# A convolution and attention block on one core: another opening order, half of a norm on ScalarE, position terms by accumulating transfer, and a Strassen product with one addition fewer

## The chip, the core and the metric

The kernel runs on one core of a Trainium2 chip. The metric is the device time in microseconds of a whole execution. Every ratio below was timed on one chip in one job, the kernels alternating. The runs belong to four such jobs, in which the kernel before took 2318.69, 2319.20, 2318.54 and 2318.88 us (medians), so times of different jobs are comparable to about 0.7 us. All runs named here count as fast: none was more than 1.5% above the fastest of its kernel. Ratios are the mean time of one kernel's fast runs over that of the other's of the same rounds, so they are not quite the ratio of the medians that are quoted.

## The reference, cut to what matters

```python
def cbs(x, w, p, pad):                       # convolution, batch norm, silu
    return jax.nn.silu(bn_eval(conv2d(x, w, pad), p))

def bot_attention(x, qkv_w, rw, rh):         # 4 heads of 64, 1024 positions
    ...
    r = (rw + rh).reshape(1, HEADS, HD, hw)  # position terms
    logits = einsum('bhdi,bhdj->bhij', q, k + r) * HD ** -0.5
    ...
t = cbs(x, cv1_w, cv1_bn, 0)                 # 1x1, 512 -> 512 channels
ys = [t[:, :C], t[:, C:]]                    # C = 256
for i in range(2):
    z = cbs(ys[-1], m_cv1_w[i], m_cv1_bn[i], 1)          # 3x3
    z = bot_attention(z, m_qkv_w[i], m_rw[i], m_rh[i])
    z = silu(bn_eval(conv2d(z, m_cv2_w[i], 0), m_cv2_bn[i]))
    ys.append(ys[-1] + z)
return cbs(concatenate(ys, axis=1), cv2_w, cv2_bn, 0)
# the result of the kernel: x + block(group_norm(x)), x of 8 images of 512 x 32 x 32
```

## The kernel before

The eight images follow each other. While one is in its first attention, the next one is loaded and normalised, and its first 1x1 convolution (cv1) begins behind that attention. The group norm is a generator, advanced one step at a time from places inside the attention. Its last step is on VectorE:

```python
def apply(cs, gm, gr):
    for c in cs:
        last = nc.vector.tensor_scalar(xts[c], xts[c], gm[:, c : c + 1], gr[:, c : c + 1],
                                       ALU.subtract, ALU.mult)
    return last
...                                       # two yields with statistics, one with the mean
yield apply(range(NX), gm, gn_rstd(dev)[0])   # the power in gn_rstd runs on GpSimd
```

An attention has four groups of four pairs. Each pair makes two logits tiles in PSUM, where the matmuls write (three buffers, shared with most other products), takes their exponential on ScalarE, sums it on VectorE, and multiplies by the values on TensorE one pair later:

```python
for i, (_, j) in enumerate(pair):
    ps = ps_big.tile([P, 2, HALF], F32, tag="big", name="l_ps")   # 3 buffers
    ...                                                           # 4 matmuls
    exp = nc.scalar.activation(pt[:, i], ps, AF.Exp, scale=SCALE)
```

From the second image on, cv1 is a Strassen product of seven products:

```python
def begin():
    ...                                        # t1, t2, t3, t4 on VectorE, two halves each
        tt(t4[:, c], t2[:, c], b21[c], ALU.subtract)
    kept["ps"] = product(a11, b11)
    kept["m1"] = to(spare("xr", 2), kept["ps"])   # to(): a copy on ScalarE
    to(y0_2, product(s4, b22))
...
def rest():
    kept["m5"] = to(spare("xr", 2), product(s1, t1))
    kept["m6"] = to(spare("x", NX), product(s2, t2))
    to(y1_2, product(s3, t3))
    to(y1_1, product(a22, t4))
```

The opening loads the first x tile, then a raw block of 3x3 weights, then the second x tile, and puts one weight transform ahead of the norm's mean on VectorE:

```python
xs = [load_x(act, 0, 0, NX)]
...
raws = {(0, 0, 0): load_raw(0, 0, 0, "k")}
xs.append(load_x(act, 0, 1, NX))
...
with tc.issue_after(shifted.ins):              # batch-norm constants
    nc.gpsimd.tensor_scalar(rstd, bnp[:, :, 3], BN_EPS, None, ALU.add)
    nc.gpsimd.tensor_tensor(rstd, rstd, mhalf[:, :NBN], ALU.pow)
    nc.gpsimd.tensor_tensor(sh, bnp[:, :, 0], rstd, ALU.mult)
    ...
```

## Time and profile before

| | before |
|---|---|
| time, median of the first three runs | 2318.8 us |
| profiled span | 2317.9 us |
| TensorE busy | 2288.9 us (99%) |
| VectorE, ScalarE, GpSimd busy | 1838.3, 987.4, 94.8 us |
| TensorE's listed waits in the first 81 us | 19.4 us in seven |
| after that | one of 0.5 us |
| after the last matmul of the last convolution started | 9.7 us |

Read it from TensorE down: an engine that is busy for 99% of the span sets the time, and the others count only where TensorE waits for them. The lines themselves are in the prediction below.

### The profile page before, as it was taken

To read this page: it belongs to the slowest core of one execution; us is meant where nothing else is said; L and a number is where in the kernel's file an instruction comes from. 1 tells how busy PE (TensorE), PEld (TensorE's weight loads), DVE (VectorE), ACT (ScalarE), POOL (GpSimd) and SP (SyncE) were. 2 spreads that over 40 slices of the span, in tenths; PEclk is the share of its full clock that TensorE was granted. 3 is DMA by queue.
4 is the path that set the end of the run, shared out by engine and by line. 5 is a ranking of instruction groups with operands and counts; after the bars stand their busy time and mean duration, and the time that the engine had idled before them with its cause. 6 is when DMAs were issued, how large, how long until landed. Compare 5 with 4: busy or idle time off the path is not lost.

```text
span 2317.9 us, 36534 instructions
## 1 busy us (share of the span) xinstructions
PE 2288.9 (99%) x14806; PEld 1174.6 (51%) x14806; DVE 1838.3 (79%) x2914; ACT 987.4 (43%) x1292; POOL 94.8 (4%) x314
## 2 busy tenths in 40 slices
PE   7999999999999999999999999999999999999998
PEld 4547346463554636446364553645436364473643
DVE  7887977888788887888788887888877988777774
ACT  2443624536244352544525345253542535335352
POOL 2000000000000000000000000000000000000000
PEclk9999999999999999999999999999999999999999
DMA  7422234041430415213161221602216031260201
GB/s 240 172 86 87 107 111 189 16 150 33 143 145 15 150 34 187 105 36 125 51 221 53 69 94 50 250 29 94 67 47 250 29 128 33 70 226 15 87 11 62
DMA packets 95521, 235.60 MB, mean 102 GB/s; under 512 B 28016, under 2 KB 50736, under 8 KB 81904
## 3 DMA queue, kind: packets, MB, share of 16 engines
q1 hardware_dynamic: 83600, 182.84, 23.1%
q0 software_dynamic: 11744, 50.34, 5.7%
q8 instruction: 119, 1.95, 0.3%
q14 instruction: 58, 0.48, 0.1%
HBM read 198.54 MB, written 34.60 MB: 101 GB/s over the span
## 4 chain that ended last, share of the span: by engine, by line
PE 96%; DVE 3%; POOL 0%; ACT 0%; DMA 0%; issue 0%; SPq 0%; DVEq 0%; POOLq 0%; ACTq 0%
PE av_ps L769 19%; PE l_ps L735 19%; PE c_ps L971 14%; PE c L1029 8%; PE p_ps L631 8%; PE x_ps L1141 6%; PE c_new L1029 6%; PE m_ps L995 5%; PE ps L387 4%; PE pv_ps L635 3%; PE s_ps L787 1%; PE p_ps L635 1%; PE s_ps L805 1%; DVE acc L755 0%; DMA raw<-in_m_cv_w_dram 0%; PE v_ps L596 0%
## 5 line engine op out<-in xcount | busy, mean ns | idle before, releaser
L739 ACT ACTIVATE pt<-l_ps 128x1024 f32<-128x1024 f32 x512 | 494.9, 1023 | 410.1 <-PE l_ps L735 385.5
L755 DVE TENSOR_TENSOR acc<-acc,pt 128x1024 f32<-128x1024 f32 x384 | 469.3, 1222 | 65.7 <-ACT pt L739 39.9
L769 PE MATMUL av_ps<-pt,vT 64*64 64x512 f32 x4096 | 486.5, 592 | 0.5 <-DVE ao L777 0.5
L735 PE MATMUL l_ps<-q,kr 64*64 64x512 f32 x4096 | 486.0, 591 | 0.0
L971 PEld LDWEIGHTS c_ps<-v_in,u 128*128 128x128 f32 x2720 | 306.0, 192 | 6.7 <-issue 6.7
L971 PE MATMUL c_ps<-v_in,u 128*128 128x128 f32 x2720 | 306.2, 275 | 0.0
L769 PEld LDWEIGHTS av_ps<-pt,vT 64*64 64x64 f32 x4096 | 159.3, 133 | 269.3 <-issue 223.1
L735 PEld LDWEIGHTS l_ps<-q,kr 64*64 64x64 f32 x4096 | 160.2, 133 | 263.2 <-issue 252.0
L453 ACT COPY m<-c_ps 128x256 f32<-128x256 f32 x96 | 35.4, 368 | 220.6 <-PE c_ps L971 218.3
L1029 PE MATMUL c_new<-t_in,ws 128*128 128x512 f32 x288 | 124.6, 592 | 0.0
L995 PE MATMUL m_ps<-ao,m_sb 128*128 128x512 f32 x256 | 112.5, 592 | 0.0
L370 ACT ACTIVATE m_kept<-m_kept,bh,sh 128x512 f32<-128x512 f32 x42 | 31.9, 806 | 146.0 <-DVE m_kept L1113 86.3
L753 DVE TENSOR_TENSOR acc<-pt 128x1024 f32<-128x1024 f32 x64 | 78.0, 1219 | 18.2 <-ACT pt L739 18.0
L1029 PEld LDWEIGHTS c_new<-t_in,ws 128*128 128x128 f32 x288 | 54.8, 190 | 68.8 <-issue 66.0
L631 PE MATMUL p_ps<-t_z,sq 128*128 128x512 f32 x180 | 87.2, 593 | 0.0
L370 ACT ACTIVATE t<-m_ps,bh,sh 128x512 f32<-128x512 f32 x64 | 48.0, 775 | 83.9 <-PE m_ps L995 82.5
L995 PEld LDWEIGHTS m_ps<-ao,m_sb 128*128 128x128 f32 x256 | 48.7, 190 | 61.2 <-issue 61.2
L1003 DVE TENSOR_TENSOR ylast<-t,ypad 128x512 f32<-128x512 f32 x32 | 22.0, 692 | 63.2 <-ACT t L370 63.2
L370 ACT ACTIVATE z<-z,bh,sh 128x512 f32<-128x512 f32 x64 | 48.6, 806 | 54.4 <-DVE z L482 54.4
L446 DVE TENSOR_TENSOR v_in<-w_rows 128x512 f32<-128x512 f32 x96 | 65.5, 683 | 0.0
L454 DVE TENSOR_TENSOR r_mid<-c_ps,m 128x256 f32<-128x256 f32 x64 | 27.0, 422 | 48.4 <-ACT m L453 48.3
L1029 PE MATMUL c<-ypad,ws 128*128 128x512 f32 x144 | 63.8, 592 | 0.0
(255 smaller groups left out, 3004.7 us busy)
## 6 DMA issues: line engine op xcount, KB each, us to landing
u<-u SPq DMA_DIRECT2D x85, 1024.0 KB
x<-in_x_dram SPq DMA_DIRECT2D x32, 512.0 KB
x_res<-in_x_dram POOLq DMA_DIRECT2D x32, 512.0 KB, 6.9
out_dram<-m_kept POOLq DMA_DIRECT2D x28, 512.0 KB, 7.4
u<-u_new POOLq DMA_DIRECT2D x12, 1024.0 KB, 4.9
w<-in_cv_w_dram SPq DMA_DIRECT2D x12, 1024.0 KB
rs<-r_dram SPq DMA_DIRECT2D x96, 128.0 KB
ws<-s SPq DMA_DIRECT2D x24, 512.0 KB
```

What stands on the lines that cost most here:

```text
L370: return nc.scalar.activation(dst, src, AF.Silu, scale=sh[:, k : k + 1], bias=bh[:, k : k + 1])
L387: last_product[0] = nc.tensor.matmul(ps[:, half, :], w_of(k), rhs_of(k, half), start=(k == begin), stop=(k == end))
L631: nc.tensor.matmul(ps[:, o, :], w[:, o, :], rhs, start=not onto, stop=True, skip_group_check=onto)
L635: nc.tensor.matmul(v[:, ts(j, P)], rhs[:, ts(j, P)], w[:, 2, :], start=j == 0 and not onto, stop=True, skip_group_check=True,)
L735: nc.tensor.matmul(ps[kh * HD : (kh + 1) * HD, hd, :], kr[r, c, o : o + HD], q[r, c, ts(half, HALF)], start=True, stop=True,)
L739: exp = nc.scalar.activation(pt[:, i], ps, AF.Exp, scale=SCALE)
L755: ins = nc.vector.tensor_tensor(accs[g], accs[g], pt[:, i], ALU.add)
L769: nc.tensor.matmul(avs[g][hd * HD : (hd + 1) * HD, kh, :], vT[r, j, o : o + HD], pt[r, i, hd, :], start=(j == 0), stop=(j == NJ - 1),)
L971: nc.tensor.matmul(ps[:, row, col, :], us[i][:, k, row, SLOT[col], :], vs[i][:, k, row, col, :], start=(k == 0), stop=(k == NM - 1),)
L995: nc.tensor.matmul(pss[oc][:, half, :], m2_sb[:, n, k, ts(oc, P)], ao[:, k, ts(half, HALF)], start=(k == 0), stop=(k == NM - 1),)
L1029: nc.tensor.matmul(ps[:, o, :], w[:, k, ts(o, P)], rhs[part][:, c, :], start=(k == 0 and not onto), stop=(k == KB - 1), skip_group_check=onto,
L1141: nc.tensor.matmul(ps[:, o, :], w[:, c, ts(o, P)], rhs[c], start=(c == 0 and not onto), stop=(c == 1), skip_group_check=onto,)
```

## The change

The intent was to start the first matmul sooner, to take work off VectorE (half of the norm's last step, additions of position terms, one addition of the Strassen sums), and to free the last output from a buffer. Cut to its core:

```diff
-    xs = [load_x(act, 0, 0, NX)]
+    xs = [load_x(act, 0, c, NX) for c in range(NX // 2)]
...
-    xs.append(load_x(act, 0, 1, NX))           # it stood behind the raw weights
...
-    with tc.issue_after(loaded.ins):
-        made = make_u(2, u_first[2][:, 0], raws[0, 0, 0])
     with tc.issue_after(read.ins):
+        with tc.issue_after(loaded.ins):
+            made = make_u(2, u_first[2][:, 0], raws[0, 0, 0])
         next(norm)
...                                        # constants: all but the power to VectorE, and behind
...                                        # the power a weight transform that stood further back
-        nc.gpsimd.tensor_tensor(sh, bnp[:, :, 0], rstd, ALU.mult)
+        nc.vector.tensor_tensor(sh, bnp[:, :, 0], rstd, ALU.mult)
...                                        # the norm's last step
-            yield apply(range(NX), gm, gn_rstd(dev)[0])
+            gr = gn_rstd(dev)[0]
+            shift = small.tile([P, 2], F32, tag="dev", name="shift")
+            nc.vector.scalar_tensor_tensor(shift, gm[:, :2], -1.0, gr[:, :2], ALU.mult, ALU.mult)
+            apply(range(2, NX), gm, gr)
+            for c in range(2):
+                nc.scalar.activation(
+                    xts[c], xts[c], AF.Identity, scale=gr[:, c : c + 1], bias=shift[:, c : c + 1]
+                )
+                yield
...                                        # position terms, built once in image 2 (make_r)
+                nc.gpsimd.dma_start(kr[:, 1, :], r_dram, accum_op=ALU.add)
...                                        # Strassen
-                to(y0_2, product(s4, b22))
+                kept["ps5"] = product(s1, [t1[:, c] for c in range(2)])
+                kept["m5"] = to(spare("xr", 2), kept["ps5"])
...
-                to(y1_2, product(s3, t3))
-                to(y1_1, product(a22, t4))
+                ps = product(s3, t3)
+                to(y1_2, ps)
+                to(y1_1, product(a22, t4, ps))      # adds onto ps
...                                        # last output
-                    t = act.tile([P, size], F32, tag="h" if n and final else "t", name="t", bufs=2)
+                    t = act.tile([P, size], F32, tag=("h", "h", "wt")[n] if final else "t", name="t", bufs=2)
```

More of the change, by code (lines that the diff above doesn't have):

```diff
@@ L243, in make_sq, with make_r @@
             nc.gpsimd.dma_start(sq_dram[n][:, 2 * h : 2 * h + 2], t)
+    r_dram = [tc.dram_tile([P, HW], F32, name=f"r{n}") for n in range(N)]
+    def make_r(n):
+        r = act.tile([P, F, F], F32, tag="xr", name="r_new", bufs=2)
+        nc.vector.tensor_tensor(
+            r, rw_sb[:, n, 1, :].unsqueeze(1).to_broadcast([P, F, F]),
+            rh_sb[:, n, 1, :].unsqueeze(2).to_broadcast([P, F, F]), ALU.add,
+        )
+        nc.gpsimd.dma_start(r_dram[n], r.rearrange("p a b -> p (a b)"))
     def load_sq(n):
@@ L551, in apply @@
                 for c in cs:
-                    last = nc.vector.tensor_scalar(
+                    nc.vector.tensor_scalar(
                         xts[c], xts[c], gm[:, c : c + 1], gr[:, c : c + 1], ALU.subtract, ALU.mult
                     )
-                return last
             stats(range(NX // 2))
@@ L562, in group_norm @@
             yield
-            yield apply(range(NX), gm, gn_rstd(dev)[0])
+            gr = gn_rstd(dev)[0]
[5 more added lines that the diff above has]
+                    xts[c], xts[c], AF.Identity, scale=gr[:, c : c + 1], bias=shift[:, c : c + 1]
+                )
+                yield
         def project(n, z):
@@ L610, in first_sum, with project_strassen @@
             return t
-        def project_strassen(n, z, sq, t):
+        def project_strassen(n, z, sq, t, r_dram=None):
             q = act.tile([P, NM, HW], F32, tag="q", name="q")
@@ L704, in later, with attention_fast @@
             def later():
-                for half in range(NH):
-                    add_r(1, half)
+                if r_dram is None:
+                    for half in range(NH):
+                        add_r(1, half)
+            if r_dram is not None:
+                nc.gpsimd.dma_start(kr[:, 1, :], r_dram, accum_op=ALU.add)
             return q, kr, vT, later
-        def attention_fast(n, z, at, behind, sq=None, t=None):
-            q, kr, vT, later = (*project(n, z), None) if sq is None else project_strassen(n, z, sq, t)
+        def attention_fast(n, z, at, behind, sq=None, t=None, r_dram=None):
+            q, kr, vT, later = (*project(n, z), None) if sq is None else project_strassen(n, z, sq, t, r_dram)
             behind.get(-1, lambda: None)()
@@ L1162, in begin @@
                     tt(t3[:, c], b22[c], b12[c], ALU.subtract)
-                    tt(t4[:, c], t2[:, c], b21[c], ALU.subtract)
+                    tt(t4[:, c], b21[c], t2[:, c], ALU.subtract)
                 kept["ps"] = product(a11, b11)
                 kept["m1"] = to(spare("xr", 2), kept["ps"])
-                to(y0_2, product(s4, b22))
+                kept["ps5"] = product(s1, [t1[:, c] for c in range(2)])
+                kept["m5"] = to(spare("xr", 2), kept["ps5"])
             def go_on():
@@ L1173, in rest @@
             def rest():
-                t1, t2, t3, t4 = ([t[:, c] for c in range(2)] for t in kept["t"])
-                kept["m5"] = to(spare("xr", 2), product(s1, t1))
+                _, t2, t3, t4 = ([t[:, c] for c in range(2)] for t in kept["t"])
+                to(y0_2, product(s4, b22, kept["ps5"]))
                 kept["m6"] = to(spare("x", NX), product(s2, t2))
-                to(y1_2, product(s3, t3))
-                to(y1_1, product(a22, t4))
+                ps = product(s3, t3)
+                to(y1_2, ps)
+                to(y1_1, product(a22, t4, ps))
             def add_y0():
@@ L1182, in add_y0 @@
                 tt(y0_2, y0_2, kept["m1"], ALU.add)
-                tt(y0_2, y0_2, kept["m5"], ALU.add)
             def add_y1():
                 tt(y1_2, y1_2, kept["m1"], ALU.add)
-                tt(y1_1, y1_2, y1_1, ALU.subtract)
+                tt(y1_1, y1_1, kept["m1"], ALU.add)
                 tt(y1_2, y1_2, kept["m5"], ALU.add)
@@ L1302 @@
         begin(Y_ORDER[2], range(NX // 2))
-    with tc.issue_after(shifted.ins):
-        nc.gpsimd.tensor_scalar(rstd, bnp[:, :, 3], BN_EPS, None, ALU.add)
+    with tc.issue_after(made.ins), tc.issue_after(shifted.ins):
+        nc.vector.tensor_scalar(rstd, bnp[:, :, 3], BN_EPS, None, ALU.add)
         nc.gpsimd.tensor_tensor(rstd, rstd, mhalf[:, :NBN], ALU.pow)
-        nc.gpsimd.tensor_tensor(sh, bnp[:, :, 0], rstd, ALU.mult)
-        nc.gpsimd.tensor_tensor(bh, bnp[:, :, 2], sh, ALU.mult)
-        nc.gpsimd.tensor_tensor(bh, bnp[:, :, 1], bh, ALU.subtract)
+        made = make_u(0, u_first[0][:, 1], raws[0, 0, 1])
+    with tc.issue_after(made.ins):
+        nc.vector.tensor_tensor(sh, bnp[:, :, 0], rstd, ALU.mult)
+        nc.vector.tensor_tensor(bh, bnp[:, :, 2], sh, ALU.mult)
+        nc.vector.tensor_tensor(bh, bnp[:, :, 1], bh, ALU.subtract)
         for at in bn_m1:
-            nc.gpsimd.tensor_scalar(sh[:, at : at + NM], sh[:, at : at + NM], -1 / 12, None, ALU.mult)
-    with tc.issue_after(made.ins):
-        made = make_u(0, u_first[0][:, 1], raws[0, 0, 1])
-    with tc.issue_after(made.ins), tc.issue_after(applied.ins):
+            last = nc.vector.tensor_scalar(sh[:, at : at + NM], sh[:, at : at + NM], -1 / 12, None, ALU.mult)
+    with tc.issue_after(last.ins), tc.issue_after(applied.ins):
         for i in (1, 2):
@@ L1411 @@
         behind = {g: ahead for g in range(NG)} | {NG: first, NG + 1: second}
+        behind[NG - 1, 1] = lambda: next(norm, None)
         if b > 0:
@@ L1415 @@
             behind[-1] = lambda: make(1, 0, range(PAIRS))
-        ao, check = s.attention_fast(0, z, b * N * NM * NH, behind, sq.get(0), t)
+        if b == 1:
+            behind |= {(NG - 1, n + 1): lambda n=n: (next(norm, None), make_r(n)) for n in range(N)}
+        ao, check = s.attention_fast(0, z, b * N * NM * NH, behind, sq.get(0), t, r_dram[0] if b > 1 else None)
         made = None
@@ L1482 @@
             behind |= {(1, 1): six[3], (2, 1): six[4]}
-        ao, check = s.attention_fast(1, z, (b * N + 1) * NM * NH, behind, sq.get(1), t)
+        ao, check = s.attention_fast(1, z, (b * N + 1) * NM * NH, behind, sq.get(1), t, r_dram[1] if b > 1 else None)
         ylast = act.tile([P, NM, HW], F32, tag="v", name="ylast")
```

## The prediction

> **What bounds the kernel now.** I began with the page: TensorE is busy 2288.9 of 2317.9 us, so at most 29 us of the span is not matmul, whatever the other engines do. Next the view of waits for TensorE, which says where those 29 us are.
>
> ```profile
> span 2317.9 us, 36534 instructions
> PE 2288.9 (99%) x14806; PEld 1174.6 (51%) x14806; DVE 1838.3 (79%) x2914; ACT 987.4 (43%) x1292; POOL 94.8 (4%) x314
> ```
>
> ```profile
> PE gm_ps L497 <- DVE mv L490: 11.0, 1, 11.0
> PE ps L387 <- ACT x L537: 2.7, 1, 2.7
> PE c_ps L971 <- DVE u_new L341: 2.4, 1, 2.4
> PE gv_ps L497 <- DVE dev L509: 0.9, 1, 0.9
> PE ps L387 <- ACT z L370: 0.9, 1, 0.9
> ```
>
> Columns: total wait, number of waits, longest. Every one happens once, in the first 81 us; in the seven images after that TensorE never waits 0.5 us. The remaining 9 us follow the last matmul. So VectorE's 79% and ScalarE's 43% cost nothing in the middle: work taken off VectorE there gains nothing, and work put on another engine can only lose.
>
> The chain that ended last gives the opening, piece by piece (start, length):
>
> ```profile
> 1.49 6.55 DMA raw<-in_m_cv_w_dram
> 9.41 1.26 DVE st L489 x2
> 15.47 5.49 PE ps L387 x6
> 27.04 3.04 POOL rstd L1305
> 30.16 4.58 POOL sh L1306
> 35.35 1.45 ACT ypad L370 x2
> 36.83 0.69 DVE w_tmp L423
> 67.16 5.78 PE c_ps L971 x28
> ```
>
> A raw weight block, loaded ahead of the second x tile, holds that tile's statistics to 9.4. The batch-norm constants take GpSimd from 26.3 to 35.3. Then VectorE runs without a gap from 36.83 to 67.16 (row transforms, weight transforms of the second output half), and TensorE waits on it. Last, the table by stretches; the columns that count are TensorE's and the granted clock before the DMA share:
>
> ```profile
> 0.00:11.00 11.00, 0.00 (x0) 0.00 (x0) 4.23 (x9) 2.10 (x3) 1.93 (x20) 1.00 0.78 257
> 61.90:67.10 5.20, 2.05 (x10) 1.56 (x10) 5.20 (x15) 1.52 (x2) 0.00 (x0) 0.83 0.40 117
> 67.10:73.00 5.90, 5.84 (x31) 5.84 (x32) 3.94 (x12) 0.00 (x0) 1.06 (x2) 0.57 0.65 267
> ```
>
> After the waits of 61.9 to 67.1 the clock falls: 28 matmul passes take 5.78 us there against 0.112 us a pass elsewhere, a further 2.6 us.
>
> **What the Trainium skill says.** "TensorE: Matmul & The Clock Gate", Part 1, says TensorE drops to half clock after an idle window of about 3.4 us and returns after a busy one; the trace agrees (0.57 above). The same page, under "Architectural detail", calls ScalarE's and VectorE's queues strict FIFO; the order of the trace agrees, though in the kernel before no ScalarE instruction stands in the wrong place. "ScalarE: Activation LUTs", "What ACT_TABLE_LOAD costs", gives 186 ns + 0.833 ns per element, 93 ns for each per-partition operand, and says back-to-back ones overlap by 93 ns; for 512 elements with scale and bias that is 0.80 us, and the trace has 0.806 for that silu. For 1024 it gives an estimate of 1.22 us, two in 2.35. "GPSIMD Engine Reference", "Key points", says GpSimd shares SBUF interfaces with VectorE; that fits 4.58 us for a 128x16 multiply beside a busy VectorE, 0.22 us when VectorE was idle.
>
> **The change, part by part.** The instruction order of the changed program (no times in it) decides much here.
>
> *Front.* x tile 2 is now loaded directly behind tile 1. 0.52 MB at the 257 GB/s above is 2.0 us, so it can be used at 4.38 + 2.0 = 6.4; statistics 1.5, then as before to the first big matmul (10.90 to 15.47 = 4.57): 12.4, 3.0 earlier. The constants go to VectorE except the power: VectorE reaches them after the second mean. In the new order the read of the second variance stands before most of a weight transform, so VectorE idles some 1.7 us there; I get row transforms starting at about 32.9 against 36.83 (VectorE, not silu, ends last). From there to the last weight transform TensorE needs for the second output half it has to do the 30.3 us it did before (36.83 to 67.16) plus 0.7 us, two more 384-element transforms less one small one being pulled in front: 64.0, 3.2 earlier. But the new order also puts the first transform of that half late: TensorE reaches it at about 55.0 and gets it at 58.9. One wait of 3.9 us replaces three smaller ones, so the clock should fall once more, for about as long. Gain of the front at the first attention: **3.3 us**.
>
> *Half of the norm's last step on ScalarE.* VectorE saves two of four 1024-element steps (2.98 us for four) in seven images: no gain, it was not waited for. ScalarE gets two activations, and the order places both directly behind the row-sum copy and ahead of the last four exponentials of the attention. They wait for the mean's shift, which needs GpSimd's power. In the second block of image 2:
>
> ```profile
> 431.86 0.38 ACT L793 COPY s_row<-s_ps 128x256 f32<-128x256 f32 x1
> 434.32 1.94 ACT L739 ACTIVATE pt<-l_ps 128x1024 f32<-128x1024 f32 x2 [2.08 <-PE l_ps L735]
> 434.41 1.04 POOL L517 TENSOR_TENSOR gr<-gr,mhalf 128x4 f32<-128x4 f32 x1 [2.69 <-DVE gr L516]
> 435.48 2.98 DVE L552 TENSOR_SCALAR x<-x,gm,gr 128x1024 f32<-128x1024 f32 x4 [1.16 <-POOL gr L517]
> 436.59 1.96 PE L735 MATMUL l_ps<-q,kr 64*64 64x512 f32 x16
> ```
>
> The power ends at 435.45, the shift at 435.65; ScalarE can start at 435.7, two activations take to 438.0, and only then comes the exponential that before began at 434.32; it ends at 439.0. Logits have three PSUM buffers: the second half of the last logits, at 436.59 + 0.86 = 437.45 before, needs the one that this exponential reads. TensorE waits 437.45 to 439.0, 1.55 us, and later steps do not win it back. Seven images (all but the last have a norm behind the attention): **10.9 us lost**.
>
> *Position terms by transfer.* Twelve attentions lose four additions on VectorE: no gain. The accumulating transfer starts when the last of the projections is done, and the second pair's logits come two groups, some 29 us, later; a 512 KB load took 6.9 us. Hidden. Building the terms costs VectorE two 1024-element additions once, in the second image, before the sums for the first product: about **1.1 us lost**, once.
>
> *Strassen.* Still seven products and six copies. One VectorE addition (1.22 us) less in six images: no gain. But the last product now accumulates onto a buffer that is being copied out (1.01 us); five matmuls of the next stage (ten passes of 0.112) are put between. Wait left: 0.04 + 1.01 + 0.03 + latency against 1.12, about 0.13 us; six times, **0.8 us lost**.
>
> *End.* The last block's first half gets another buffer and does not wait for an output transfer (before: 2308.80, 2.44 us after the issue of that transfer). The remaining additions and the three issues move by about **0.8 us** earlier.
>
> Sum: 2318.8 - 3.3 - 0.8 + 10.9 + 1.1 + 0.8 = **2327.5 us**.
>
> **The rivals.** (a) The ScalarE work fits into its idle time (it is busy 57% per pair of exponentials): then only front and end count and the time is about 2316. For it: 1.49 us idle before most exponentials. Against: the two stand back to back and behind a value that is not there until 435.6. (b) TensorE's wait of 1.55 us, if it falls within one clock window, drops the clock each time; up to 1.7 to 3.4 us more in each image, 2340 to 2350. Against: 0.91 us idle at 80 dropped nothing, and the fall at 65 followed 3.9 us of waits. (c) The front's 3 us are lost to the late weight transform and the clock: 2330 to 2331. (d) An accumulating transfer that is several times slower than a plain one would delay the third group of logits in twelve places; it would need over 25 us to show.
>
> **Range and chances.** The activation's length (1.0 to 1.3 us) moves the loss by about 4 us, the front is good for 1 to 5.5 us. I give (a) one chance in ten and (b) one in ten. That makes 2317 to 2334 for 8 in 10. A difference of 2% is 46 us, and no case reaches it: 0.01 faster, 0.97 within 2%, 0.02 slower.
>
> **What would show it.** In the view of waits: a new line of logits waiting for an exponential, some 7 times 1.5 us; ScalarE's norm step waiting for the shift, seven times about 3.5 us. In the opening: first big matmul at 12.4, batch-norm constants ready by 28 and no 4.58 us multiply on GpSimd, row transforms at 33, a wait of some 4 us at 55 to 59 and again a clock of one half. Half the VectorE norm instructions; the second image's product waiting about a microsecond. I am wrong if the logits do not wait, if the front gives more than 6 us, or if attention's third group waits for a transfer.

## The result, and the profile after

The changed kernel took 2328.93 us (median of 6 runs, 2327.23 to 2329.41) against 2318.69 us (6 runs, 2317.74 to 2320.06) for the kernel before: a ratio of 1.0043, with a 95% interval of 1.0030 to 1.0056. It is within 2%, and slower by some 10 us. The profiled spans differ by 10.0 us.

The head of the page of the changed kernel:

```profile
span 2327.9 us, 36547 instructions
PE 2291.4 (98%) x14806; PEld 1167.4 (50%) x14806; DVE 1800.5 (77%) x2861; ACT 1002.7 (43%) x1306; POOL 100.9 (4%) x322
```

VectorE lost 37.8 us of work, as intended, and the program became longer. So look at what TensorE waits for (total us, number, longest):

```profile
PE l_ps L755 <- ACT pt L759: 9.3, 7, 1.3
...
PE c_ps L991 <- DVE u_new L355: 3.2, 1, 3.2
...
PE x_ps L1162 <- DVE t_x L1181: 0.7, 1, 0.7
...
PE c L1049 <- DVE ao L797: 0.3, 1, 0.3
```

The first line is new and happens seven times, once for each image that has a norm behind its first attention. ScalarE's own waits name the cause, seven times too:

```profile
ACT x L577 <- DVE shift L574: 24.1, 7, 3.4
```

The second block of image 2 in order of time (start, length), the same place that the prediction shows of the kernel before:

```profile
431.11 1.04 POOL L527 TENSOR_TENSOR gr<-gr,mhalf 128x4 f32<-128x4 f32 x1 [2.69 <-DVE gr L526]
432.18 0.16 DVE L574 SCALAR_TENSOR_TENSOR shift<-gm,gr 128x2 f32<-128x2 f32 x1 [1.16 <-POOL gr L527]
432.26 1.53 DVE L562 TENSOR_SCALAR x<-x,gm,gr 128x1024 f32<-128x1024 f32 x2
432.38 2.37 ACT L577 ACTIVATE x<-x,shift,gr 128x1024 f32<-128x1024 f32 x2 [3.43 <-DVE shift L574]
434.66 3.74 ACT L759 ACTIVATE pt<-l_ps 128x1024 f32<-128x1024 f32 x4
435.71 1.09 PE L755 MATMUL l_ps<-q,kr 64*64 64x512 f32 x8 [1.32 <-ACT pt L759]
```

ScalarE stands idle for 3.43 us. The first 2.08 us it would have waited for logits anyway, as in the kernel before; for the other 1.35 us logits are ready to be taken, but the two activations are at the head of its queue and their shift is not there. They then take 2.37 us, and only at 434.66 does the first of four exponentials start; TensorE resumes when that one has freed its buffer.

The opening in three views: a line of the chain that ended last, TensorE's row in order of time, and the table by stretches for two clock windows (length; busy time and number of instructions of TensorE, weight loads, VectorE, ScalarE, GpSimd; granted clock; transfer share; GB/s):

```profile
23.73 3.17 POOL rstd L1327
```

```profile
43.26 11.55 PE L991 MATMUL c_ps<-v_in,u_new 128*128 128x128 f32 x102
57.98 0.71 PE L991 MATMUL c_ps<-v_in,u_new 128*128 128x128 f32 x4 [3.17 <-DVE u_new L355]
```

```profile
55.24:58.65 3.41, 0.67 (x4) 0.52 (x4) 3.41 (x11) 0.02 (x1) 0.00 (x0) 1.00 0.00 0
58.65:62.06 3.41, 3.12 (x15) 3.08 (x15) 3.41 (x9) 1.50 (x2) 0.53 (x1) 0.50 0.56 231
```

The first big matmul starts at 12.22 us (before: 15.47), the power ends at 26.9, the row transforms start at 32.0 (before: 36.83), the long wait is there from 54.8 to 58.0, and the clock halves for one window of 3.41 us (before: 6.83 us, from 65.34 to 72.17). The first attention starts at 92.08 instead of 97.35.

**Where the 10 us went.** TensorE runs almost the same matmuls in both kernels, so each one's start can be compared with its twin's. This drift (after minus before) is a staircase that can be read directly:

| piece | drift in us |
|---|---|
| at the first logits of image 1 | -5.27 |
| last logits of the first attention, images 1 to 7 | +1.56 each, 10.9 in all |
| from there to the second attention, images 2 to 7 (Strassen) | +0.35 each, 2.1 in all |
| at the same place in image 2, once more | +1.05 |
| end of image 1 | +0.4 |
| at the last logits of image 8 | 9.11 |
| from the last convolution's last matmul to the end | +0.96 |

After the opening the drift falls by no more than 0.05 us from one logits matmul to the next: what TensorE loses in an image it keeps. In the experiments I use the *body*, the drift between the first logits of image 1 and the last of image 8, because it leaves out the opening. That one scattered by 2 us from run to run under the same code: in the nine runs that have it whole its drift was -4.6 to -6.6 us, with a median of -5.7. The body of the changed kernel is 9.11 + 5.27 = 14.38 us.

### The profile page after: what moved, and what is told of

The parts are those of the page before. It is cut to its first block, busy times and chain, and to the rows that moved or that the text cites. A ratio compares the mean times of both kernels' runs of the same rounds, so it can differ in the third digit from the quotient of the medians.

```text
span 2327.9 us, 36547 instructions
## 1 busy us (share of the span) xinstructions
PE 2291.4 (98%) x14806; PEld 1167.4 (50%) x14806; DVE 1800.5 (77%) x2861; ACT 1002.7 (43%) x1306; POOL 100.9 (4%) x322
## 4 chain that ended last, share of the span: by engine, by line
PE 92%; DVE 4%; issue 1%; ACT 1%; DMA 1%; POOL 1%; SPq 0%; DVEq 0%; POOLq 0%; ACTq 0%
PE l_ps L755 17%; PE av_ps L789 17%; PE c_ps L991 14%; PE c L1049 8%; PE p_ps L648 8%; PE c_new L1049 6%; PE x_ps L1162 6%; PE m_ps L1015 5%; PE ps L397 4%; PE pv_ps L652 3%; PE p_ps L652 1%; PE s_ps L807 1%; DVE acc L775 1%; ACT pt L759 1%; PE s_ps L825 1%
## 5 line engine op out<-in xcount | busy, mean ns | idle before, releaser
L1162 PE MATMUL x_ps<-t_x,sw 128*128 128x512 f32 x144 | 64.1, 594 | 0.7 <-DVE t_x L1181 0.7
```

Source lines behind the costliest of these rows:

```text
L1162: nc.tensor.matmul(ps[:, o, :], w[:, c, ts(o, P)], rhs[c], start=(c == 0 and not onto), stop=(c == 1), skip_group_check=onto,)
```

## The experiments

Theory: the 10.9 us come from the place of two activations in ScalarE's queue. Rivals: from the amount of ScalarE's work, or from another part of the change. Each part was also taken alone. The diffs are cut to what matters.

### The norm back on VectorE (e1_norm_vector)

```diff
-            shift = ...                                   # and the two activations
-            apply(range(2, NX), gm, gr)
+            apply(range(NX), gm, gr)
```

> The changed kernel with all four steps of the norm back on VectorE, everything else kept. Theory (a value not yet ready at the head of ScalarE's queue): the matmul order of before and after drifts apart by 1.56 us in each of seven images at the last logits, so 2328.9 - 10.9 = 2318.0 us (2317.0 to 2319.0), and the line of logits waiting for an exponential is gone from TensorE's waits. Rival (these waits come from the transfer of position terms or from the Strassen reordering): 2327 to 2329 and the line stays.

Measured: 2318.92 us (5 runs, 2317.82 to 2319.38), and no wait of the logits. The body fell from 14.38 to 4.31 us, by 10.1: the seven steps of 1.56 became zero, but image 2 lost 0.94 more, in two waits of its second product for VectorE's sums (0.78 and 0.68 us), most likely because VectorE has two norm steps more ahead of them. So the norm's part is confirmed as a cause, and the transfer and Strassen are excluded as causes of that line.

### The same activations, two exponentials later (e2_norm_behind)

```diff
             apply(range(2, NX), gm, gr)
-            for c in range(2):
-                nc.scalar.activation(...)
-                yield
+            yield
+            with tc.issue_after(exps[-1].ins):            # the last exponential so far
+                for c in range(2):
+                    nc.scalar.activation(...)
+            yield
```

> The changed kernel; the same two activations on ScalarE in each of seven images, but queued behind the third pair of exponentials of the last group instead of in front of it; VectorE's order is identical. Theory (the wait for the shift at the head of the queue costs, not the work): the shift is ready when that pair ends, the last pair is 0.9 us later and nothing on TensorE needs it sooner: no logits wait, 2318.0 us (2317 to 2319). Rival (ScalarE has no room for 2.4 us more in this attention wherever it stands): at least 0.87 us an image stays, 2324 us or more.

Measured: 2317.75 us (5 runs, 2317.10 to 2318.04). The same block of image 2:

```profile
428.80 1.94 ACT L763 ACTIVATE pt<-l_ps 128x1024 f32<-128x1024 f32 x2 [2.08 <-PE l_ps L759]
...
429.96 0.16 DVE L576 SCALAR_TENSOR_TENSOR shift<-gm,gr 128x2 f32<-128x2 f32 x1 [1.16 <-POOL gr L527]
...
430.62 2.37 ACT L581 ACTIVATE x<-x,shift,gr 128x1024 f32<-128x1024 f32 x2
...
432.89 1.93 ACT L763 ACTIVATE pt<-l_ps 128x1024 f32<-128x1024 f32 x2
```

The 2.37 us of work are the same, and ScalarE no longer waits in front of them: the shift ends at 430.12, half a microsecond before they begin. The last two exponentials start 4.09 us after the two before them instead of 3.43, and nobody needs them sooner; the seven steps in the drift are gone (0.02 us or less), and the body is 2.89 us. It was the place in the queue, not the work. This is the run that decides, since VectorE's order is the same in both kernels.

### One activation instead of two (e3_norm_one)

```diff
-            apply(range(2, NX), gm, gr)
-            for c in range(2):
+            apply(range(1, NX), gm, gr)
+            for c in range(1):
```

> The changed kernel with one activation of the norm on ScalarE and three steps on VectorE. Theory: the exponential starts one activation (1.19 us) sooner, so the logits' wait falls from 1.33 to about 0.14 us, and the drift per image from 1.56 to 0.37: 2328.9 - 7 x 1.19 = 2320.6 us (2319.5 to 2321.8). Rival 1 (loss in proportion to the activations): half of 10.9, 2323.5 us. Rival 2 (the 3.4 us wait for the shift alone sets the loss): 2327 us or more.

Measured: 2320.82 us (5 runs, 2319.50 to 2321.48); the logits' waits fell to 1.3 us in seven, 0.2 each, and the step to 0.42 us. The loss is not proportional to the activations: 1.56 for two and 0.42 for one. It is the delay of the exponential less a fixed slack: counted from 2.08 us of idle on, which the kernel before has there too, the exponential starts 3.63 us late with two activations and 2.50 us with one, and 3.63 - 1.56 and 2.50 - 0.42 both leave about 2.1 us. I put this slack down to the third PSUM buffer, but no run changes the number of buffers. One activation less moved it by 1.14 us, which is half of 2.37 within 0.05.

### The opening alone (e4_front_only, e9_front_again)

The kernel before with the changed loads, order and constants, and nothing else.

> The kernel before with the front of the change alone. Theory (trace: the first attention starts 92.08 instead of 97.35, nothing later in the image depends on the front): 2318.7 - 5.3 = 2313.4 us (2312.5 to 2314.5), which beats both. Rival (as I had predicted, the late weight transform and the clock eat all but the earlier loads): 2315.4 us.

> The same kernel as e4_front_only, again, now on one chip with the next run. Theory (the constants on VectorE gather TensorE's small waits for weight transforms into one of 3.4 us, after which the clock falls to half for 3.4 us in every kernel that has them): 2313.5 us and 1.0 to 1.6 us more than the next run. Rival (the difference of e4 and e8 was a difference of chips or of the clock window's phase): equal within 0.4 us.

Measured: 2313.62 us (5 runs, 2312.33 to 2314.53), ratio to the kernel before 0.9977 (0.9964 to 0.9991), and again 2314.09 us (5 runs, 2313.21 to 2314.63), 0.9981. The body of the first was -0.04 us, so nothing later was touched. Against the medians of the kernel before in the same jobs (2319.20 and 2318.88) the opening gained 5.6 and 4.8 us, not the 3.3.

### The opening with the constants left on GpSimd (e8_front_no_constants, e10_no_constants_again)

Only the first two hunks of the diff above: both x tiles first, and the weight transform behind the read of the second variance.

> The kernel before with the x tiles loaded first and the read of the second variance ahead of the weight transform, but the batch-norm constants still on GpSimd. Theory (two parts add up): first big matmul at 12.2 as with the whole front, gain 3.2 us: 2318.7 - 3.2 = 2315.5 us; the other 2.1 us of the front's 5.3 come from the constants on VectorE. Rival 1 (the constants are the whole bound of the start of the row transforms): no gain, 2318.5. Rival 2 (the constants on VectorE buy nothing): 2313.5.

> The same kernel as e8_front_no_constants, again. Theory: 2312.3 us; no wait of TensorE over 1.5 us after the first 40 us and no stretch of half clock between 20 and 2300 us. Rival: as e9_front_again, with a stretch of half clock.

Measured: 2312.47 us (5 runs, 2311.80 to 2313.11), ratio 0.9973 (0.9960 to 0.9987), and again 2312.88 us (5 runs, 2312.31 to 2313.62), ratio 0.9976 (0.9962 to 0.9990), on the same chip as e9's 2314.09. I had expected 2315.5 for it at first: that was a miss by 3 us, and it is below both rivals too. It is the fastest kernel, faster than both given ones. In the one job that holds both openings (e9 and e10) it is faster than the one with the constants on VectorE by 1.2 us, as expected there, though the two ranges overlap by 0.4 us; e4 and e8 ran in different jobs, and gained 5.6 and 6.1 us on the kernel before of their own. TensorE's row in the opening of the first of the two runs:

```profile
43.14 11.55 PE L970 MATMUL c_ps<-v_in,u_new 128*128 128x128 f32 x102
54.95 0.71 PE L970 MATMUL c_ps<-v_in,u_new 128*128 128x128 f32 x4 [0.27 <-DVE u_new L344]
56.62 4.31 PE L970 MATMUL c_ps<-v_in,u_new 128*128 128x128 f32 x32 [0.95 <-DVE u_new L345]
62.24 6.30 PE L970 MATMUL c_ps<-v_in,u_new 128*128 128x128 f32 x54 [1.32 <-DVE u_new L344]
```

Three waits of 0.27, 0.95 and 1.32 us stand where the changed kernel has one of 3.17, and the clock stays at full speed: in both runs the records show no half clock from 18 us to the last matmul, while all nine profiled runs with the constants on VectorE have a stretch of it. From the first of these matmuls to the first of the next stage it takes 25.2 us, against 26.9 in the changed kernel and 28.9 before. VectorE's order differs in two things between the two openings: the constants, and the first weight transform of the second half, which the built order finishes behind more of the row transforms when the constants are on VectorE. These runs do not separate the two. The reason for moving the constants was gone by then: with the first two hunks alone GpSimd's multiply takes 0.24 us instead of 4.57, and the row transforms start at 31.30 us, sooner than the 31.95 of the changed kernel.

### The loads alone (e11_loads_only)

Only the first hunk.

> The kernel before with only the two x tiles loaded ahead of the raw weights; the weight transform stands ahead of the copy of the mean on VectorE, as its order shows. Theory (the loads alone gain nothing, because the transform's raw weights now land about 2 us later, near 10 us, and the mean's copy waits behind three 256-element steps to about 11.3): first big matmul at 15 to 16 us, 2318 us. Rival (the x tile's landing was the whole bound): first big matmul at 12.2, 2312.5 to 2315 us.

Measured: 2314.53 us (5 runs, 2314.33 to 2316.14), first big matmul at 13.90 us. The time lies in the rival's range and the first matmul between the two, so my theory was wrong in size: the mean's copy did wait behind the weight transform, but only to 10.14 us. More than half of the gain at the first matmul is lost to that (15.47 before, 11.99 in e8), and it is what the second hunk brings back. The first matmul is also the smaller part of this kernel's gain: it comes 1.57 us sooner than before, but the first attention 5.34 us. Here too the records show no half clock between 18.6 us and the last matmul, against 6.83 us of it before, as in e8.

### The additions back, without the accumulating transfer (e5_adds_back)

```diff
-        ao, check = s.attention_fast(0, z, ..., r_dram[0] if b > 1 else None)
+        ao, check = s.attention_fast(0, z, ...)           # the same for the second attention
-        if b == 1:                                        # make_r: build and store the terms
-            ...
```

> The changed kernel with the second pair's position terms added on VectorE again (four additions in each of twelve attentions; no stored terms, no accumulating transfer). Theory: the additions cost nothing, so what comes back is the building of the terms in image 2 (1.13 us of drift, the wait of its product for VectorE) and the end of the program: GpSimd's last drain took 2.93 us in every kernel with the accumulating transfers and 2.03 in the two without, with a 0.90 against a 0.67 us semaphore step ahead of it. 2328.9 - 1.1 - 1.0 = 2326.8 us (2325.8 to 2327.8), and the drain 2.03 us. Rival 1 (the 48 additions are worth something): 2329 or more. Rival 2 (the drain has another cause): drain 2.93, about 2327.8.

Measured: 2327.26 us (5 runs, 2325.84 to 2327.84), inside the range. The extra 1.05 us of image 2 are gone (the body is 13.07), so 48 additions on VectorE were worth nothing that shows. And the end: GpSimd's last drain in the trace took 2.03 us here, as in all six other runs without accumulating transfers, and 2.93 us in all six with them; the semaphore step ahead of it took 0.67 against 0.90. From the start of the last matmul to the end it was 9.3 to 10.0 us without and 10.4 to 11.0 us with. The kernels with them issue 100 transfers from GpSimd instead of 86 (twelve accumulating ones and two stores of the terms), and e5 takes all fourteen out: whether the accumulation or the number lengthens the drain is not shown.

### The old Strassen order (e6_strassen_back)

The three functions of the kernel before, in the changed kernel.

> The changed kernel with the old Strassen first stage. Theory (the trace: 0.08 us of drift at the next convolution and 0.26 at the last product, in each of six images): 2328.9 - 6 x 0.34 = 2326.9 us (2325.9 to 2327.9), and the drift per image falls from 1.90 to 1.56. Rival (my recorded 0.13 us an image): 2328.1 us, drift 1.77. The matmul starts of the trace decide, as the times scatter by a microsecond.

Measured: 2325.95 us (5 runs, 2325.43 to 2326.74), lower than the theory's value by 0.9. The 0.35 us in each image are gone, and so is, unexpectedly, the 1.05 us of image 2, although the terms are still built there: the body is 11.32, lower by 3.06, about 6 x 0.35 + 1.05. Image 2 at its second product, first in the changed kernel, then here:

```profile
443.70 1.12 PE L1162 MATMUL x_ps<-t_x,sw 128*128 128x512 f32 x2
445.51 2.84 PE L1162 MATMUL x_ps<-t_x,sw 128*128 128x512 f32 x6 [0.68 <-DVE t_x L1181]
```

```profile
442.10 3.60 PE L1162 MATMUL x_ps<-x,sw 128*128 128x512 f32 x8
```

The new order takes s1 times t1 as its second product, and t1 is a sum that VectorE makes just before; the old order takes s4 times b22 there, which needs no sum. Building the terms delays VectorE in both. It is only seen when the product behind it needs VectorE. The cost belongs to neither part alone.

### The last product in its own buffer (e7_strassen_own_buffer)

```diff
-                ps = product(s3, t3)
-                to(y1_2, ps)
-                to(y1_1, product(a22, t4, ps))
+                to(y1_2, product(s3, t3))
+                to(y1_1, product(a22, t4))
...
-                tt(y1_1, y1_1, kept["m1"], ALU.add)
+                tt(y1_1, y1_1, y1_2, ALU.add)
```

> The changed kernel, new Strassen order and accumulation of the fifth product kept, but the last product in its own PSUM buffer, and its sum with the third made on VectorE. Theory (the last product waits for the copy of the buffer it adds to): the 0.26 us a image at that place go, drift 1.64, 2328.9 - 1.6 = 2327.3 us. Rival (the earlier fifth product or the changed order costs it): drift stays 1.90 and 2328.9 us.

Measured: 2327.72 us (5 runs, 2325.62 to 2329.03), too wide to tell by itself, but the drift per image at this place fell from 0.35 to 0.09, as expected. In this run the clock stood at half for two windows in the opening, one more than in the changed kernel's profile, which the body leaves out; it is 12.99. The place in the changed kernel:

```profile
470.10 1.28 PE L991 MATMUL c_ps<-v_in,u 128*128 128x128 f32 x10
471.37 3.70 PE L1162 MATMUL x_ps<-t_x,w 128*128 128x512 f32 x8
```

The ten small passes start on time and the product that adds onto the copied buffer starts 1.27 us after them, 0.15 more than ten passes of 0.112; from its first start to the next stage it then takes 3.53 us, against 3.44 in the kernel before. No wait is listed for it, as it is too short; only the comparison of starts shows it.

## Why the prediction was right or wrong

The class was right, the time was 2328.9 against 2327.5 predicted, and the range held. By its steps:

- **What bounds the kernel.** Right: 37.8 us less on VectorE gained nothing that any run shows, and every loss on TensorE stayed.
- **Norm on ScalarE, 10.9 us lost.** Right in mechanism and size: 1.56 us in each of seven images against 1.55 worked out, two activations in 2.37 us against the estimated 2.35, the same line of waits. The runs added what the argument could not show: moving the same work behind one pair of exponentials costs nothing.
- **Front, 3.3 us gained.** Mis-sized: it was 5.3 in the profiled pair, and 5.6 and 4.8 in the times of the opening alone. The first matmul came 3.25 us sooner, as worked out (3.0), and the late transform held TensorE to 57.98, which was given as 58.9. Two terms failed. TensorE was not held by weight transforms until 64.0: it waited for none after 58.98. And the clock did not fall "for about as long": it fell for one window of 3.41 us instead of two (in e7, with the same opening, for two). The clock and a shorter sum of waits (3.17 + 0.29 against 0.69 + 2.44 + 0.77) are the other 2 us. The hunk with the constants costs about 1 us (1.2 in the job that ran both openings) instead of gaining: with them on GpSimd the kernel is faster.
- **Position terms, 1.1 us lost once.** The size was right (1.05), and no attention waited for a transfer. The step "before the sums for the first product" had half of the cause: it is the second product, and without the Strassen change nothing would have waited.
- **Strassen, 0.8 us lost.** Mis-sized: 0.35 us an image and 2.1 in all, not 0.13 and 0.8. Of it 0.26 are the shared buffer; 0.09 come with the new order.
- **End, 0.8 us gained.** Wrong. The step that failed is that the last block's first half had waited for an output transfer. The two kernels' rows of VectorE at the end show that both start behind TensorE (the bracket is the idle time before and who ended it):

```profile
2308.80 1.35 DVE L1236 TENSOR_TENSOR t<-ps,part 128x512 f32<-128x512 f32 x3 [1.83 <-PE ps L387]
```

```profile
2317.91 1.35 DVE L1258 TENSOR_TENSOR t<-ps,part 128x512 f32<-128x512 f32 x3 [1.93 <-PE ps L397]
```

  It starts 0.63 us after the last matmul's start in both. In place of a gain, GpSimd's longer drain made the end about 1 us later.
- **Not foreseen:** 0.4 us at the end of image 1, where a scaling on VectorE stood behind a late small transfer. It was 0.0 to 0.5 us in the other runs, so I count it as scatter.

The sum as measured: -5.3 + 10.9 + 1.05 + 2.1 + 0.4 + 0.96 = 10.1, against 10.0 of the two spans. The record came within 1.4 us because errors of -2.0 (front), +1.8 (end), +1.3 (Strassen) and +0.4 partly cancelled; that part is luck. The term of 10.9 us is not.

Of the rivals, (a) fell as a forecast but was right about ScalarE's room: the work does fit, in another place. (b) fell: the granted clock stayed at full speed from 62 us to the last matmul. (c) and (d) fell.

## What to carry to other kernels

An engine with idle time can still be the wrong place for work if it takes its instructions in order: ask where in its queue the new instruction stands and whether its inputs are there at that moment, and queue it behind the work that others wait for. Taking work off an engine that nobody waits for gains nothing, and it can cost if the reordering makes a product depend on that engine's latest result. Compare the starts of the same matmuls in two traces: the staircase gives each part of a change its size, to a tenth of a microsecond, where times scatter by one.

## What the Trainium skill lacked or had wrong

- "TensorE: Matmul & The Clock Gate", Part 1, speaks of one idle window before half clock, and of frequent short idles that make the clock swing, but gives no busy share at which it falls. Here windows that were partly busy were enough: 0.67 us busy of 3.41 in the changed kernel and 0.97 before (61.93 to 65.34), so the prediction's "the trace agrees" was too simple. A window with 2.08 us busy of 3.41 did not lower it (e8, 58.75 to 62.16, counted in steps of 3.41 us from a change of the clock on record). And a window with 2.64 us busy at half clock (65.34 to 68.75 before) did not restore it, one with 3.12 did (58.65 to 62.06 in the changed kernel). The page says that the window is free-running and the phase differs between runs; the runs agree: the same opening had half clock for 3.41 or for 6.83 us.
- "DMA: Bandwidth & Descriptors", "SWDGE vs HWDGE vs iDMA", gives GpSimd as the engine for accumulating transfers and no cost at the end of the program. In six of six runs with them GpSimd's last drain took 2.93 us, in seven of seven without them 2.03 us. It is open why, and whether the accumulation or the fourteen more transfers do it.
- "SBUF — State Buffer", "Who interferes with whom", says that a VectorE instruction with two SBUF inputs contends with a GpSimd one that reads SBUF and that the order of issue decides who is blocked, but not how long a run of VectorE instructions can hold a GpSimd one back. The same 128x16 multiply on GpSimd took 4.57 us in the kernel before and ended just after VectorE's unbroken run (34.73 against 34.64 us); in e8, also beside a busy VectorE, it took 0.24 us. The prediction's reading, busy or idle, was too simple; what lets it in is open.
